# Inverse standard deviations as a power on GpSimd, a second layer's row statistics taken where its input is written, and a minimum in place of an accumulated Relu

## The chip, the cores and the metric

The kernel runs on one core of one Trainium2 chip. The metric is device time in microseconds (us), the median of several executions. Engine names are those of the profile: PE is TensorE (matrix multiply), DVE is VectorE, ACT is ScalarE, POOL is GpSimd, and SP only issues DMAs.

## What is computed

Two graph layers follow each other on `x` of shape (8, 2048, 256) in float32, with one adjacency matrix `adj` (2048, 2048) of integers. Both start from `h = relu(layernorm(x))` and add their result to `x`:

```python
def layer0(x):                      # 4 heads of 64
    h = max(layernorm(x), 0)
    q, k, v = h @ Wq.T + bq, h @ Wk.T + bk, h @ Wv.T + bv
    s = clip(q k^T / 8, -10, 10); s = where(adj == 0, -10, s)
    # softmax over each chunk of 256 keys by itself, chunks added up
    ctx = sum over 8 chunks of softmax(s_chunk) @ v_chunk
    o = ctx @ Wo.T + bo + h
    return x + layernorm(o) * gamma + beta
def layer1(x):                      # 4 heads of 64
    h = max(layernorm(x), 0)
    q = h @ W
    e = leaky_relu(q.a_src + q.a_dst)    # for every pair of rows
    return x + elu(softmax(where(adj > 0, e, -9e15)) @ q)
```

Each layernorm needs, for every row, the mean, the variance and the inverse standard deviation 1/sqrt(variance + 1e-5). There are three of them: of `x` (layer 0's input), of `o` (inside layer 0), and of layer 0's result (layer 1's input). The kernel uses a mask with 0 and 1 in it, and therefore also finds out whether any entry of `adj` is negative; if so, a slower function, `gat_layer`, computes the second layer anew. With the given inputs it doesn't run.

## The kernel before

**Layer 0.** For each of 8 batches `b`, 2048 query rows are cut into four blocks `qb` of 512, and the keys into eight chunks `c` of 256. One (b, qb, c) is a *step*; there are 256. A step multiplies queries with keys on PE (L396, into PSUM buffers `big`, of which there are two), applies clip and mask on DVE (L404, into `E`), takes the exponential on ACT (L410), adds the two key tiles on POOL (L680), sums over keys on PE (L427), weighs the values on PE (L416), and scales the result with the inverse sums on DVE (L452, into `c`, or `acc` in a block's first step). The inverse sums go by way of L434 (copy), a DMA, L441 (reciprocal on DVE), and DMAs through DRAM that spread them over the partitions (`r<-inv`). POOL adds `c` to `acc` (L454).

**Layer 1.** For each batch there are four *passes* (two pairs of heads, two halves of 1024 query rows); a pass has 16 *rounds* `jt` of 128 keys. A round makes two `e` tiles of 128x1024 on DVE (L761), weighs them on PE (L772), scales every other one on ACT (L874), adds the next one to it on POOL (L878), and sums on PE (L784). `e` and `E` share ten buffers. At the end of a pass, `ending` divides and applies elu (L805 to L835).

**Work on the side.** Beside this, generators stand in a list `aside`. Each call of `advance()` lets each generator do a piece; a `yield` without a value ends that call, `yield True` lets the next generator go on. Layer 0 calls `advance` twice a step, layer 1 once a round. So a piece's place in each engine's queue follows from the number of yields before it[...]. If a pass needs what a generator hasn't finished, `drain` runs all that is left of it at once. The generators that matter:
- `make_limit(qb)` makes the mask: `adj` is loaded in eight parts, cast to bf16 on ACT, transposed on PE (L260) and written by DVE (L261).
- `batch(b)` takes row statistics of `x[b]` in `statistics`, then for each block normalizes (L160), transposes (L171), and projects to q, k, v (L297, L191). For batch 0 it does this before the first step, block by block.
- `finish(b, qb, acc)` ends a block of layer 0 during the next block: `o` from `x` (L466, L469), the output projection (L479) added to it (L487), row statistics (`mv2`), normalization (L501), then gamma, beta and `x` on POOL (L512), and a DMA to `x1[b]` in DRAM (L513). `o` has two buffers, which it shares with `for_sums`.
- `preparation(b)` makes what layer 1 needs of batch `b`: statistics, normalized transposed rows, attention terms (L559 to L617, with a trip through DRAM), and eight tiles of `qn` (L191 on PE, L629 on DVE). For batch 0 it runs in the last batch of layer 0; for the others during the passes of the batch before.

**Row statistics** are two DVE instructions a row tile, L47 and L48 in `row_stats`, and give mean and variance in `mv`. Then `roots` and `offsets` make the inverse standard deviation `rstd` and `off = -mean * rstd`: a square root on ACT, a copy with a factor of -1 on ACT, a reciprocal on DVE, a multiplication on POOL (L127, L128, L131, L132). They act on 4 columns (a block) or 16 (a batch). [...]ACT_TABLE_LOAD instructions stand at L127 and at the next exponential.

The functions that the change touches, with the line numbers of the profile:

Of the kernel before, what the change touches and what calls it, by code (L numbers as in the profile page):

```python
# [8 lines left out]
F32 = mybir.dt.float32  # L9
BF16 = mybir.dt.bfloat16  # L10
I32 = mybir.dt.int32
FP8 = mybir.dt.float8e5
AF = mybir.ActivationFunctionType
ALU = mybir.AluOpType
PSUM = bass.MemoryType.PSUM

P = 128
EPS = 1e-5
# [26 lines left out]
def row_stats(nc, small, mv, row):  # L45
    st = small.tile([P, 6], F32, tag="st", name="st")
    nc.vector.bn_stats(st, row)  # L47
    nc.vector.bn_aggr(mv, st)  # L48
# [3 lines left out]
def layers(  # L52
# [18 lines left out]
    nc = tc.nc  # L71
    B, N, F = x.shape
# [4 lines left out]
    NQB = N // QB  # L77
    NKT = N // P
    NCH = N // 256
    NT = QB // P  # L80
    FC = F // P

    const = ctx.enter_context(tc.tile_pool(name="const_l", bufs=1))
    big = ctx.enter_context(tc.tile_pool(name="big", bufs=2))
    small = ctx.enter_context(tc.tile_pool(name="small", bufs=2))
# [27 lines left out]
                coming = load(rows, blk + 1)  # L113
            yield xb

    eps = const.tile([P, 1], F32, tag="eps", name="eps")
    nc.vector.memset(eps, EPS)

    def norms():

        mv = small.tile([P, NKT, 2], F32, tag="mv", name="mv")
        rstd = small.tile([P, NKT], F32, tag="rstd", name="rstd", bufs=3)
        off = small.tile([P, NKT], F32, tag="off", name="off", bufs=3)
        return mv, rstd, off

    def roots(mv, rstd, off, of):
        nc.scalar.activation(rstd[:, of], mv[:, of, 1], AF.Sqrt, bias=eps)  # L127
        nc.scalar.activation(off[:, of], mv[:, of, 0], AF.Copy, scale=-1.0)  # L128

    def offsets(rstd, off, of):  # L130
        nc.vector.reciprocal(rstd[:, of], rstd[:, of])  # L131
        nc.gpsimd.tensor_tensor(off[:, of], off[:, of], rstd[:, of], ALU.mult)  # L132

    def statistics(rows):

        mv, rstd, off = norms()
        for blk, xb in enumerate(ahead(rows)):
            if blk == 0:
                yield True
                yield True  # L140
            for t in range(NT):
                row_stats(nc, small, mv[:, blk * NT + t, :], xb[:, t, :])
                if t % 2:
                    yield True
        of = slice(0, NKT)
        roots(mv, rstd, off, of)
        yield True
        offsets(rstd, off, of)
        yield True
        yield True  # L150
        return rstd, off
# [50 lines left out]
    here = [0]  # L202
# [16 lines left out]


    limit = const.tile([P, NQB, NKT, QB], FP8, tag="limit", name="limit")
    below = const.tile([P, NQB, 2 * NT], F32, tag="below", name="below")
    made = []

    identb = const.tile([P, P], BF16, tag="identb", name="identb")
# [8 lines left out]
    def make_limit(qb):  # L234
        parts = [(t, half) for t in range(NT) for half in range(2)]

        def fetch(k):
            t, half = parts[k]
            q0 = qb * QB + t * P
            raw = adj_in[(qb * len(parts) + k) % 3]  # L240
            nc.sync.dma_start(raw, adj[q0 : q0 + P, half * 1024 : (half + 1) * 1024])
            return raw

        def cast(k):

            m = masks[:, k % 2, :]
            nc.scalar.activation(m, raws[k], AF.Relu, scale=-1.0, accum_out=below[:, qb, k : k + 1])
            nc.scalar.copy(m, raws[k])
            return m

        raws = [fetch(k) for k in range(3)]
        yield True
        m = cast(0)
        yield True
        for k, (t, half) in enumerate(parts):
            if k + 3 < len(parts):
                raws.append(fetch(k + 3))
            ps = aux(BF16).rearrange("p (k q) -> p k q", q=P)
            for j in range(8):
                nc.tensor.transpose(ps[:, j, :], m[:, j * P : (j + 1) * P], identb)  # L260
            nc.vector.tensor_scalar(  # L261
                limit[:, qb, half * 8 : (half + 1) * 8, t * P : (t + 1) * P],
                ps, 0.0, 0.5, ALU.not_equal, ALU.subtract, saturate=False,
            )
            if k + 1 < len(parts):
                m = cast(k + 1)
            else:
                made.append(qb)
            yield
# [49 lines left out]
    def batch(b):  # L319
        qkv[b] = ([], [], [])  # L320
        if b == 0:
            mv, rstd, off = norms()
            norm_of[b] = rstd, off
            for blk, xb in enumerate(ahead(x[b])):
                if blk == 0:
                    yield True
                for t in range(NT):
                    row_stats(nc, small, mv[:, blk * NT + t, :], xb[:, t, :])
                of = slice(blk * NT, (blk + 1) * NT)
                roots(mv, rstd, off, of)  # L330
                offsets(rstd, off, of)
                yield from block(b, blk, xb, *qkv[b])
        else:
            norm_of[b] = yield from statistics(x[b])
            for blk, xb in enumerate(ahead(x[b])):
                yield from block(b, blk, xb, *qkv[b])
# [119 lines left out]
    def finish(b, qb, acc):  # L456
        rstd, off = norm_of[b]
        xb = load(x[b], qb)
        n = here[0]

        while here[0] < n + 1:
            yield False
        o = big.tile([P, NT, F], F32, tag="o", name="o")
        for t in range(NT):
            i = qb * NT + t
            nc.scalar.activation(  # L466
                o[:, t, :], xb[:, t, :], AF.Relu, scale=rstd[:, i : i + 1], bias=off[:, i : i + 1]
            )
        nc.gpsimd.tensor_tensor(o, o, bcast(brow["o"], 1, NT), ALU.add)  # L469
        yield True  # L470
        while here[0] < n + 2:
            yield False
        mv = small.tile([P, NT, 2], F32, tag="mv2", name="mv2")
        for two in range(NT // 2):
            ps = aux().rearrange("p (t f) -> p t f", t=2)
            for u in range(2):
                t = 2 * two + u
                for part in range(2):
                    nc.tensor.matmul(  # L479
                        ps[:, u, :],  # L480
                        acc[:, part, t * P : (t + 1) * P],
                        wT["o"][:, part, :],
                        start=(part == 0),
                        stop=(part == 1),
                    )
            mine = o[:, 2 * two : 2 * two + 2, :]
            nc.vector.tensor_tensor(mine, mine, ps, ALU.add)  # L487
            yield
            for u in range(2):
                t = 2 * two + u  # L490
                row_stats(nc, small, mv[:, t, :], o[:, t, :])
        rstd2 = small.tile([P, NT], F32, tag="rstd2", name="rstd2")
        off2 = small.tile([P, NT], F32, tag="off2", name="off2")
        roots(mv, rstd2, off2, slice(0, NT))
        yield True
        offsets(rstd2, off2, slice(0, NT))
        n = here[0]
        while here[0] < n + 1:
            yield False
        for t in range(NT):  # L500
            nc.scalar.activation(  # L501
                o[:, t, :], o[:, t, :], AF.Identity,
                scale=rstd2[:, t : t + 1], bias=off2[:, t : t + 1],
            )
            if t == 1:
                yield True
        for k, more in enumerate((bcast(brow["gamma"], 1, NT), bcast(brow["beta"], 1, NT), xb)):
            yield True
            n = here[0]
            while here[0] < n + 1:  # L510
                yield False
            nc.gpsimd.tensor_tensor(o, o, more, ALU.add if k else ALU.mult)  # L512
        nc.gpsimd.dma_start(  # L513
            x1[b][qb * QB : (qb + 1) * QB, :].rearrange("(t p) f -> p t f", p=P), o
        )
        yield True


    shared = {}
    least = const.tile([P, B, H], F32, tag="least", name="least")  # L520
    spans = const.tile([P, B, 2 * H], F32, tag="spans", name="spans")

# [21 lines left out]
    def preparation(b):  # L544

        w, wa = shared["w"], shared["wa"]
        norm = yield from statistics(x1[b])

        er = const.tile([P, NQB, P], F32, tag="wv", name="er")
        hTs = []  # L550
# [73 lines left out]
        for blk in range(NQB):  # L624
            q = big.tile([P, NT, F], F32, tag="kv", name="qn", bufs=12)
            for two in range(2):
                ps = sides(w, two, hTs[blk])
                n = blk * NT + 2 * two
# [57 lines left out]
    for n in range(-2, len(steps)):  # L686
# [4 lines left out]
        if n >= 0:  # L691
            b, qb, c = steps[n]
# [160 lines left out]
    for s, (k, jt) in enumerate(rounds):  # L853
        here[0] = len(steps) + s // 4
        b, hp, half = passes[k]
# [46 lines left out]
    nc.vector.tensor_reduce(worst[:, 0:1], spans, mybir.AxisListType.XY, ALU.max)  # L902
    nc.vector.tensor_reduce(worst[:, 1:2], least, mybir.AxisListType.XY, ALU.min)
    nc.vector.tensor_reduce(worst[:, 2:3], inverse_most, mybir.AxisListType.X, ALU.max)
    nc.vector.tensor_reduce(worst[:, 3:4], below, mybir.AxisListType.XY, ALU.max)
    for k, (bound, op) in enumerate(
        ((60.0, ALU.is_gt), (-12.0, ALU.is_lt), (1e26, ALU.is_gt), (0.0, ALU.is_gt))
    ):
        nc.vector.tensor_scalar(bad[:, k : k + 1], worst[:, k : k + 1], bound, None, op)
    ps = aux()  # L910
# [290 lines left out]
```

## Time and profile before

| | |
|---|---|
| median of 3 executions | 4478.36 us (4476.7 to 4484.94) |
| the profiled execution | 4470.84 us, of which the span of instructions 4469.0 us |
| busy share of the span | PE 95%, POOL 73%, DVE 71%, ACT 61% |
| granted PE clock | 0.991 |
| ACT_TABLE_LOAD | 95 of 1283 ns |
| DMA | 262 MB, mean 59 GB/s |
| layer 0, with its start | to about 2903 us |
| layer 1 | from there to 4469 us |

Shares are means over stages with different limits. PE's busy time is modelled, since matmuls are pipelined and their ends are not recorded. The page's groups are written `line engine operation out<-in xcount | busy us, mean ns of one | idle us of the engine just before, and what ended it`.

### The profile page before, as it was taken

To read this page: it belongs to the slowest core of one execution; us is meant where nothing else is said; L and a number is where in the kernel's file an instruction comes from. 1 tells how busy PE (TensorE), PEld (TensorE's weight loads), DVE (VectorE), ACT (ScalarE), POOL (GpSimd) and SP (SyncE) were. 2 spreads that over 40 slices of the span, in tenths; PEclk is the share of its full clock that TensorE was granted. 3 is DMA by queue.
4 is the path that set the end of the run, shared out by engine and by line. 5 is a ranking of instruction groups with operands and counts; after the bars stand their busy time and mean duration, and the time that the engine had idled before them with its cause. 6 is when DMAs were issued, how large, how long until landed. Compare 5 with 4: busy or idle time off the path is not lost. (4 is left out here: it accounts for less than half of the span.)

```text
span 4469.0 us, 73769 instructions
## 1 busy us (share of the span) xinstructions
PE 4235.0 (95%) x28598; PEld 1462.8 (33%) x28598; DVE 3157.1 (71%) x3736; ACT 2712.5 (61%) x3454; POOL 3275.9 (73%) x1558
## 2 busy tenths in 40 slices
PE   6799999999999999999999999989999999999998
PEld 3233333323323333333333333323233332323332
DVE  1775566566565565575565566588989889898987
ACT  4766556656655665665656557565647566565755
POOL 0477787787677777777777777777877777787877
PEclk8999999999999999999999999999999999999999
DMA  2421121111121121121111122121221212122111
GB/s 70 140 62 44 43 66 47 43 56 56 35 64 54 37 66 44 46 64 44 47 55 50 40 64 61 44 100 50 72 63 60 78 57 86 52 74 62 59 55 35
DMA packets 295000, 262.03 MB, mean 59 GB/s; under 512 B 96240, under 2 KB 245488, under 8 KB 294640
## 3 DMA queue, kind: packets, MB, share of 16 engines
q1 hardware_dynamic: 290032, 240.45, 18.8%
q0 software_dynamic: 4608, 16.78, 1.0%
q8 instruction: 226, 3.70, 0.3%
q14 instruction: 134, 1.10, 0.1%
HBM read 218.83 MB, written 36.18 MB: 57 GB/s over the span
## 5 line engine op out<-in xcount | busy, mean ns | idle before, releaser
L680 POOL TENSOR_TENSOR add<-E 128x1024 f32<-128x1024 f32 x512 | 1201.3, 2369 | 721.9 <-PE sums L427 532.1
L410 ACT ACTIVATE E<-E 128x1024 f32<-128x1024 f32 x1024 | 1080.5, 1057 | 827.3 <-DVE E L404 809.6
L404 DVE SCALAR_TENSOR_TENSOR E<-big,limit 128x1024 f32<-128x1024 f32 x1024 | 1203.7, 1217 | 521.6 <-PE big L396 515.5
L761 DVE SCALAR_TENSOR_TENSOR e<-near,far,limit 128x1024 f32<-128x1024 f32 x1024 | 1240.0, 1273 | 23.2 <-ACT near L750 9.8
L878 POOL TENSOR_TENSOR t<-t,e 128x1024 f32<-128x1024 f32 x448 | 1054.4, 2387 | 246.0 <-ACT t L874 210.4
L416 PE MATMUL both<-E,v 128*32 128x512 f32 x8192 | 1037.7, 601 | 59.8 <-DVE c L452 42.3
L772 PE MATMUL acc<-e,qn 128*32 128x512 f32 x8192 | 1060.7, 597 | 24.4 <-DVE e L761 13.5
L396 PE MATMUL big<-qT,kT 64*128 64x512 f32 x4096 | 1032.3, 620 | 11.8 <-DVE E L404 11.8
L874 ACT ACTIVATE t<-e,quot 128x1024 f32<-128x1024 f32 x512 | 561.2, 1142 | 313.5 <-PE den L784 173.0
L396 PEld LDWEIGHTS big<-qT,kT 64*128 64x128 f32 x4096 | 351.6, 187 | 572.0 <-issue 348.8
L454 POOL TENSOR_TENSOR acc<-acc,c 128x1024 f32<-128x1024 f32 x224 | 532.9, 2379 | 3.6 <-DVE c L452 3.6
L452 DVE TENSOR_TENSOR c<-both,r 128x1024 f32<-128x1024 f32 x224 | 274.2, 1224 | 345.9 <-PE both L416 157.1
L416 PEld LDWEIGHTS both<-E,v 128*32 128x32 f32 x8192 | 214.7, 109 | 752.3 <-issue 572.8
L772 PEld LDWEIGHTS acc<-e,qn 128*32 128x32 f32 x8192 | 259.2, 109 | 591.5 <-issue 451.1
L784 PE MATMUL den<-t,for_sums 128*32 128x512 f32 x2048 | 347.6, 595 | 30.6 <-POOL t L878 29.8
L427 PE MATMUL sums<-add,ones 128*32 128x512 f32 x2048 | 269.1, 592 | 0.2 <-POOL add L680 0.2
L434 ACT COPY s<-sums 128x512 f32<-128x512 f32 x256 | 148.4, 580 | 75.5 <-PE sums L427 71.3
L784 PEld LDWEIGHTS den<-t,for_sums 128*32 128x32 f32 x2048 | 79.2, 110 | 223.1 <-issue 113.3
L191 PE MATMUL aux<-w,hT 128*128 128x256 f32 x512 | 127.6, 392 | 22.6 <-DVE qn L629 22.6
L160 ACT ACTIVATE h<-x,off,rstd 128x256 f32<-128x256 f32 x256 | 139.2, 593 | 4.3 <-DMA x<-in_x_dram 2.3
L297 PE MATMUL aux<-hT,wq 128*128 128x512 f32 x256 | 135.7, 658 | 2.7 <-ACT hT L172 2.7
L479 PE MATMUL aux<-wo,acc 128*128 128x256 f32 x512 | 128.2, 393 | 0.0
(117 smaller groups left out, 3033.8 us busy)
## 6 DMA issues: line engine op xcount, KB each, us to landing
r<-inv SPq DMA_DIRECT2D x1024, 64.0 KB
x<-in_x_dram SPq DMA_DIRECT2D x92, 512.0 KB
x<-x SPq DMA_DIRECT2D x64, 512.0 KB
es<-er SPq DMA_DIRECT2D x64, 512.0 KB
adj_in<-in_adj_dram SPq DMA_DIRECT2D x32, 512.0 KB
x<-o POOLq DMA_DIRECT2D x32, 512.0 KB, 3.9
xh<-x SPq DMA_DIRECT2D x64, 256.0 KB
out_dram<-xh SPq DMA_DIRECT2D x64, 256.0 KB
```

What stands on the lines that cost most here:

```text
L396: nc.tensor.matmul(ps[:, hh, :], ks[kt // NT][own, hp, (kt % NT) * P : (kt % NT + 1) * P], qs[qb][own, hp, :], start=True, stop=True,)
L404: nc.vector.scalar_tensor_tensor(e, ps, -0.5, bcast(limit[:, qb, kt, :], 1, 2), ALU.max, ALU.min)
L410: nc.scalar.activation(e, e, AF.Exp, scale=0.25 * EDGE)
L416: nc.tensor.matmul(both[32 * h : 32 * h + 32, part, :], vs[kt // NT][:, kt % NT, mine], es[h // 2][:, h % 2, :], start=first, stop=not first,)
L452: nc.vector.tensor_tensor(to, both, bcast(r, 1, 2), ALU.mult)
L454: nc.gpsimd.tensor_tensor(acc, acc, to, ALU.add)
L680: nc.gpsimd.tensor_tensor(both, first[hp], second[hp], ALU.add)
L761: nc.vector.scalar_tensor_tensor(e, near[hh], far[:, jt, h : h + 1], limit[:, 2 * half : 2 * half + 2, jt, :], ALU.max, ALU.min,)
L772: nc.tensor.matmul(acc[32 * q : 32 * q + 32, blk, :], qn[jt // NT][:, jt % NT, hp * P + 32 * q : hp * P + 32 * q + 32], es[q // 2][:, blk, :],
L784: nc.tensor.matmul(den[32 * q : 32 * q + 32, :], for_sums[:, m, 2 * hp + q // 2, :], ts[q // 2][:, q % 2, :], start=(m == 0 and k == 0), s ...
L874: nc.scalar.activation(t, now[hh], AF.Copy, scale=quot[:, jt // 2, h : h + 1])
L878: nc.gpsimd.tensor_tensor(ts[hh], ts[hh], now[hh], ALU.add)
```

## The change

Three edits. First, `roots` makes `rstd` and `off` on POOL alone: it adds epsilon, raises to the power -0.5 (the exponent is a constant tile of one column, read again for each column), multiplies the mean by -1, and multiplies by `rstd`. `offsets` is gone, and with it one yield in `statistics`. Second, `finish` takes the statistics of layer 0's result from the SBUF tile `o`, one step after the last L512, into a tile `moments` that holds all batches; `preparation` no longer loads `x1[b]` for statistics and begins with `roots`. Third, the cast of `adj` no longer counts negative entries with an accumulating Relu on ACT; DVE takes the minimum of each part, and the end of the kernel compares the smallest with 0.

```diff
-    eps = const.tile([P, 1], F32, tag="eps", name="eps")
-    nc.vector.memset(eps, EPS)
+    power = const.tile([P, 1], F32, tag="power", name="power")
+    nc.vector.memset(power, -0.5)
...
     def roots(mv, rstd, off, of):
-        nc.scalar.activation(rstd[:, of], mv[:, of, 1], AF.Sqrt, bias=eps)
-        nc.scalar.activation(off[:, of], mv[:, of, 0], AF.Copy, scale=-1.0)
-
-    def offsets(rstd, off, of):
-        nc.vector.reciprocal(rstd[:, of], rstd[:, of])
+        nc.gpsimd.tensor_scalar(rstd[:, of], mv[:, of, 1], EPS, None, ALU.add)
+        nc.gpsimd.tensor_tensor(rstd[:, of], rstd[:, of], power.broadcast_to([P, of.stop - of.start]), ALU.pow)
+        nc.gpsimd.tensor_scalar(off[:, of], mv[:, of, 0], -1.0, None, ALU.mult)
         nc.gpsimd.tensor_tensor(off[:, of], off[:, of], rstd[:, of], ALU.mult)
...
@@ statistics
-        of = slice(0, NKT)
-        roots(mv, rstd, off, of)
-        yield True
-        offsets(rstd, off, of)
+        roots(mv, rstd, off, slice(0, NKT))
         yield True
         yield True
...
@@ make_limit, cast
-            nc.scalar.activation(m, raws[k], AF.Relu, scale=-1.0, accum_out=below[:, qb, k : k + 1])
             nc.scalar.copy(m, raws[k])
+            nc.vector.tensor_reduce(
+                below[:, qb, k : k + 1], raws[k], mybir.AxisListType.X, ALU.min
+            )
...
@@ finish, after the DMA to x1
         yield True
+        n = here[0]
+        while here[0] < n + 1:
+            yield False
+        for t in range(NT):
+            row_stats(nc, small, moments[:, b, qb * NT + t, :], o[:, t, :])
+            if t % 2:
+                yield True
...
+    moments = const.tile([P, B, NKT, 2], F32, tag="moments", name="moments")
...
@@ preparation
-        norm = yield from statistics(x1[b])
+        rstd, off = norms()
+        roots(moments[:, b], rstd, off, slice(0, NKT))
+        norm = rstd, off
+        yield True
```

In the first batch and in `finish`, the calls of `offsets` are dropped as well. `mv` is now a tile of its own with one buffer, `below` holds integers, and at the end one more reduction and one copy of a single column bring the smallest entry to the comparison.

More of the change, by code (lines that the diff above doesn't have):

```diff
@@ L114, in ahead @@
             yield xb
-    eps = const.tile([P, 1], F32, tag="eps", name="eps")
-    nc.vector.memset(eps, EPS)
+    power = const.tile([P, 1], F32, tag="power", name="power")
+    nc.vector.memset(power, -0.5)
     def norms():
-        mv = small.tile([P, NKT, 2], F32, tag="mv", name="mv")
         rstd = small.tile([P, NKT], F32, tag="rstd", name="rstd", bufs=3)
         off = small.tile([P, NKT], F32, tag="off", name="off", bufs=3)
-        return mv, rstd, off
+        return rstd, off
     def roots(mv, rstd, off, of):
-        nc.scalar.activation(rstd[:, of], mv[:, of, 1], AF.Sqrt, bias=eps)
-        nc.scalar.activation(off[:, of], mv[:, of, 0], AF.Copy, scale=-1.0)
-    def offsets(rstd, off, of):
-        nc.vector.reciprocal(rstd[:, of], rstd[:, of])
+        nc.gpsimd.tensor_scalar(rstd[:, of], mv[:, of, 1], EPS, None, ALU.add)
+        nc.gpsimd.tensor_tensor(rstd[:, of], rstd[:, of], power.broadcast_to([P, of.stop - of.start]), ALU.pow)
+        nc.gpsimd.tensor_scalar(off[:, of], mv[:, of, 0], -1.0, None, ALU.mult)
         nc.gpsimd.tensor_tensor(off[:, of], off[:, of], rstd[:, of], ALU.mult)
     def statistics(rows):
-        mv, rstd, off = norms()
+        rstd, off = norms()
+        mv = small.tile([P, NKT, 2], F32, tag="mv", name="mv", bufs=1)
         for blk, xb in enumerate(ahead(rows)):
@@ L221, in layers @@
     limit = const.tile([P, NQB, NKT, QB], FP8, tag="limit", name="limit")
-    below = const.tile([P, NQB, 2 * NT], F32, tag="below", name="below")
+    below = const.tile([P, NQB, 2 * NT], I32, tag="below", name="below")
     made = []
@@ L321, in batch @@
         if b == 0:
-            mv, rstd, off = norms()
+            rstd, off = norms()
+            mv = small.tile([P, NKT, 2], F32, tag="mv", name="mv", bufs=1)
             norm_of[b] = rstd, off
@@ L330, in batch @@
                 roots(mv, rstd, off, of)
-                offsets(rstd, off, of)
                 yield from block(b, blk, xb, *qkv[b])
@@ L495, in finish @@
         yield True
-        offsets(rstd2, off2, slice(0, NT))
         n = here[0]
@@ L546, in preparation @@
         w, wa = shared["w"], shared["wa"]
-        norm = yield from statistics(x1[b])
+        rstd, off = norms()
+        roots(moments[:, b], rstd, off, slice(0, NKT))
+        norm = rstd, off
+        yield True
         er = const.tile([P, NQB, P], F32, tag="wv", name="er")
@@ L904, in layers @@
     nc.vector.tensor_reduce(worst[:, 2:3], inverse_most, mybir.AxisListType.X, ALU.max)
-    nc.vector.tensor_reduce(worst[:, 3:4], below, mybir.AxisListType.XY, ALU.max)
+    lowest = small.tile([P, 1], I32, tag="lowest", name="lowest", bufs=1)
+    nc.vector.tensor_reduce(lowest, below, mybir.AxisListType.XY, ALU.min)
+    nc.vector.tensor_copy(worst[:, 3:4], lowest)
     for k, (bound, op) in enumerate(
-        ((60.0, ALU.is_gt), (-12.0, ALU.is_lt), (1e26, ALU.is_gt), (0.0, ALU.is_gt))
+        ((60.0, ALU.is_gt), (-12.0, ALU.is_lt), (1e26, ALU.is_gt), (0.0, ALU.is_lt))
     ):
```

## The prediction

> **What bounds the kernel.** I read the page first, then the windows of whole passes, then the chain of waits inside one pass, then the order of VectorE (DVE). From the page, busy tenths in 40 slices:
>
> ```profile
> PE   6799999999999999999999999989999999999998
> DVE  1775566566565565575565566588989889898987
> POOL 0477787787677777777777777777877777787877
> ```
>
> TensorE (PE) looks full from start to end. DVE changes: 5 to 7 tenths in layer 0 (to about 2903 us), 8 to 9 in layer 1. PE's nines prove little, since its matmul ends are modelled; I therefore look at how time divides where the work is periodic. In layer 1 a batch is four passes of 16 `jt` rounds. Four passes of one batch, then a pass of the last batch, which prepares nothing (columns: stretch, length, busy PE, PEld, DVE, ACT, POOL, clock, DMA share, GB/s):
>
> ```profile
> 3305.80:3355.70 49.90, 46.91 (x368) 12.59 (x363) 47.85 (x69) 25.99 (x30) 40.33 (x20) 1.00 0.28 85
> 3355.70:3397.80 42.10, 40.71 (x364) 13.38 (x368) 39.97 (x37) 34.45 (x48) 34.70 (x18) 1.00 0.31 101
> 3397.80:3442.20 44.40, 43.22 (x404) 13.88 (x400) 41.37 (x40) 32.33 (x45) 37.42 (x21) 1.00 0.20 53
> 3442.20:3499.90 57.70, 54.36 (x408) 23.01 (x404) 45.64 (x46) 26.97 (x34) 39.84 (x20) 1.00 0.13 37
> 4318.10:4360.40 42.30, 40.08 (x340) 11.59 (x332) 39.83 (x37) 25.55 (x30) 37.56 (x18) 1.00 0.18 51
> ```
>
> A bare pass is 42.3 us with DVE at 39.8. The first pass of a batch is 7.6 us longer at about the same number of matmuls (368 against 340), and the fourth 15.4 us longer. Inside the first, the timeline of DVE, and the chain of waits from 3330 to 3350 us:
>
> ```profile
> 3325.55 2.46 DVE L761 SCALAR_TENSOR_TENSOR e<-near,far,limit 128x1024 f32<-128x1024 f32 x2
> 3327.94 0.42 DVE L47 BATCH_NORM_STATS2 st<-x 128x6 f32<-128x256 f32 x1
> ...
> 3329.02 2.44 DVE L761 SCALAR_TENSOR_TENSOR e<-near,far,limit 128x1024 f32<-128x1024 f32 x2
> ...
> 3332.45 2.44 DVE L761 SCALAR_TENSOR_TENSOR e<-near,far,limit 128x1024 f32<-128x1024 f32 x2
> by line: DVE e L761 57.5%; issue 24.1%; DVE st L47 20.1%; DVE mv L48 7.2%
> ```
>
> DVE never idles here: two `e` and two row statistics every 3.43 us, where a round without them takes 2.4. The statistics stand on the path with their full length. So **layer 1 is bound by DVE**. Layer 0 is not: a plain step (start of one L452 to the next) takes 8.4 us with gapless matmuls and DVE at 6, and a step with two more PE units takes 12.24 us whatever DVE and ACT hold.
>
> **What the Trainium skill says.**
> - Perfetto Trace Analysis, Identifying the Most-Contended Engine: matmul busy time is not a good measure, since pipelined matmuls overlap. The trace agrees: PE is 95% busy in a bare pass that DVE paces.
> - ScalarE: Activation LUTs, What ACT_TABLE_LOAD costs: 1283 ns, plus 1380 ns of drain, at each switch of table set. The load agrees (1283 ns below); the drain is not to be seen here, since the instruction before ended at 1213.65 us and the load began at 1213.66.
> - VectorE: DVE Perf Modes, the perf-mode tier table: `tensor_reduce` has a 1x mode only, so 1024 elements are paid one by one.
> - GPSIMD Engine Reference, Elementwise: no price for a power; 2.6 cycles per element of a two-input add (2.37 us for 1024 here) and 12 per element for branching on data.
>
> The rows used:
>
> ```profile
> L127 ACT ACT_TABLE_LOAD x47 | 60.3, 1283 | 0.8
> L410 ACT ACT_TABLE_LOAD x40 | 51.3, 1283 | 0.7
> L132 POOL TENSOR_TENSOR off<-off,rstd 128x4 f32<-128x4 f32 x36 | 7.4, 206 | 85.2 <-DVE rstd L131 85.2
> L132 POOL TENSOR_TENSOR off<-off,rstd 128x16 f32<-128x16 f32 x15 | 3.4, 224 | 58.8 <-PE den L784 51.4 <-DVE rstd L131 7.4
> L571 DVE TENSOR_REDUCE ends<-er 128x1 f32<-128x512 f32 x8 | 5.3, 668 | 0.0
> ```
>
> **Part 1, statistics moved.** The order of the two built programs shows where they go. DVE's count of row statistics is unchanged (384), but 112 of them, those for batches 1 to 7, leave layer 1; 8 (the last two blocks of the last batch) come at its start.
> - *Layer 1, batches 1 to 6.* Gone: 8 rounds x (3.43 - 2.4) = 8.2 us. As the preparation starts about 12 rounds earlier, its eight `qn` steps (L629) stand one to a round in the third pass, where four of them were run in one go by a drain (a round of 11.3 us, 2.2 us a step). The interleaved ones cost 1.3 to 2.2 us, mean 1.8, so 4 x 0.4 = 1.6 us more. Next bound: PE in those rounds, then DVE's 42 us a pass, then POOL's 38. Sum 9.8 x 6 = **-59**.
> - *Batch 0 of layer 1*: -8.2, four late pairs +4.2, drain -1: **-5**.
> - *Last batch of layer 0*: batch 0's 16 rows leave steps that they stretch by about 1.2 us each: **-5**.
> - *DMAs*: 32 of the 64 `x<-x` loads of 512 KB go; the DMA share of the passes is 0.13 to 0.31. The rest of the preparation (four loads, six small DMAs, `roots` on POOL) moves a pass ahead, past the `es`, `xh` and `out` DMAs of other rounds on SP, which now and before wait there for POOL; the place within a pass is much the same. Zero, 2 us a batch if an `x` load is caught behind an `out`.
> - *Layer 0*: two pairs of rows for each of 30 blocks, after the reciprocal (L441) in the block's first step and after the c (L452) that ends it. At 1.08 us a pair this could be 65 us. But in the first slot DVE waits for PE anyway, 0.73 to 3.2 us in every block:
>
> ```profile
> 755.17 0.24 DVE L441 RECIPROCAL sum<-sum 128x16 f32<-128x16 f32 x1
> ...
> 756.14 2.36 DVE L404 SCALAR_TENSOR_TENSOR E<-big,limit 128x1024 f32<-128x1024 f32 x2 [0.73 <-PE big L396]
> ```
>
> and in the second slot PE has the L479 matmuls between. The step at 244.6 us already has such a pair there: it takes 9.83 us, its like without one 9.82. Also new: DVE now waits for POOL's last L512; it ends 3 to 9 us before the slot. I take 0.2 us a block and 1 us in the six blocks where statistics of the next batch sit in the same slot: **+12**; ends 0 and +65.
> - *Buffer*: `o` (two buffers) lives until these statistics. Since `for_sums` takes one earlier than before, the last two blocks' L466 on ACT now wait for DVE, with exponentials queued behind: 3 us each, **+6**; ends 0 and +15.
>
> **Part 2, power on GpSimd.** 94 of 95 table loads go (121 us of ACT), 102 small ACT activations and 51 DVE reciprocals; 153 small POOL instructions come. ACT is 52 to 82% busy in the passes above, and in layer 0 steps with a load are as long as those without (12.24 and 9.82), because PE bounds them; only steps of the six statistics batches show an excess, 0.3 to 1.6 us: **-6**. POOL pays three more instructions of 0.21 us and the power. Of the power no row exists: at least a multiply's 0.21/0.22; with the skill's 12 cycles, 16 x 12 / 1.2 GHz = 0.16 us more, an estimate of 0.4. I take 0.4; an upper end cannot be had from the page. Behind it in POOL's queue stand L680 (layer 0) and L878 (layer 1), on which PE's sums wait. Cover: the step with the four-column power lasts 10.9 to 12.24 us and holds 3 x 2.37 = 7.1 us of POOL work, so 4 us are free; at the start of a batch POOL sits idle for 4.7 to 6.8 us in the timeline (waiting for DVE's L807 or ACT's L874). So zero up to about 4 us for 4 columns and 5 us for 16, in full above that.
>
> **Part 3, minimum.** ACT loses 32 x (1.045 + 0.187) us, DVE gains 32 reductions of 1024: from 0.41 us for 256 and 0.67 for 512, 1.2 us each. Until 116.7 us DVE is busy for 20 us only, and the ACT work stands between `h` and `hT`: 4 blocks x 1.15, plus 3 x 0.85 for the roots that no longer cross four engines, plus 1: **-8**. From 116.7 to 244.6 us, 24 reductions make DVE the bound: 7 steps x 6.1 + 24 x (1.2 + 1.1) = 98 us against 93.4 now: **+7**; ends -5 and +20. The SP queue's mask loads now wait for DVE too, one reduction later.
>
> **Sum.** -59 - 5 - 5 + 12 + 6 - 6 - 8 + 7 = -58 us. The profiled execution took 4470.84 us (span 4469.0); the median shown is 4478.36, 7.5 us above. The change goes onto the median: 4420 us.
>
> **Rivals.**
> - *Layer 1 is PE's after all* (95.5% in every window): the -59 vanishes, about 4480. Against it: `e` rounds follow DVE's own sum. 5%.
> - *The moved pairs cost their full length in layer 0*: +65 for +12, about 4473. Against it: the 9.83 us step. 7%.
> - *The power is slow*, the case on the other side. With p us for 4 columns and 4p for 16, the 15 wide ones exceed their cover by 15 x (4p - 5) and eat the 58 us at p about 2.2; the 36 narrow ones follow from p = 4. At p = 4: 4478 - 58 + 165 = 4585 us, with L680 and L878 late. For it: no row; against it: POOL's other elementwise work runs at a few cycles an element. 10%.
> - *The change doesn't take the table loads away*: excluded, the built program has one.
>
> **Chances.** 0.2% (9 us) is about what a measurement of this kernel can tell from no change. Main case 78%, 4375 to 4460. With the rivals: faster 0.80, same 0.06, slower 0.14. The range reaches to 4490, past the first two rivals; slow powers beyond it are left out.
>
> **What would show it.** Right: first passes at 42 us, none with a round of 11 us, a batch of 184 instead of 194 us; one table load; powers under 1 us; the step after each block's first unchanged at 9.82 or 12.24. Wrong: first passes still at 50 (PE), steps with the new pairs at 11 us, or POOL instructions of several us at the power's line with L680 late behind them.

## The result and the profile after

| | before | after |
|---|---|---|
| median of 6 executions, us | 4478.15 | 4440.09 |
| lowest and highest, us | 4474.9, 4484.94 | 4434.26, 4445.28 |
| profiled execution (span), us | 4470.84 (4469.0) | 4443.6 (4441.7) |
| ACT_TABLE_LOAD | 95 | 1 |
| layer 1 from its first `e`: batch 0, us | 203.2 | 207.4 |
| each of batches 1 to 6, us | 194.1 | 188.6 |
| batch 7 and the end, us | 192.7 | 193.3 |

The change makes the kernel **38 us faster** (ratio 0.9913, 95% interval 0.99 to 0.9926); 58 had been forecast. Line numbers are now those of the changed kernel: `e` is L768, the weighing L779, the scaling on ACT L881, the adds on POOL L885, the sums on PE L791, `roots` L126 to L129, the exponential L407, `o` from `x` L463 and L466. The experiments have line numbers of their own.

The page's busy tenths, against those shown of before: in layer 1 (the last fourteen slices) DVE has two nines instead of five, and POOL eight digits over 7 instead of three.

```profile
PE   6799999999999999999999999989999999999998
DVE  2976666566666675675666566668888898888897
POOL 0477787787777787877777788777888788788797
```

The windows of one batch's four passes and of a bare pass after (columns as before: stretch, length, busy PE, PEld, DVE, ACT, POOL, clock, DMA share, GB/s):

```profile
3494.00:3542.00 48.00, 44.61 (x388) 14.12 (x392) 40.12 (x36) 32.00 (x44) 42.95 (x24) 1.00 0.31 89
3542.00:3586.80 44.80, 43.64 (x408) 13.98 (x400) 41.36 (x40) 32.30 (x45) 37.81 (x21) 1.00 0.19 53
3586.80:3642.40 55.60, 55.60 (x416) 22.88 (x412) 45.63 (x46) 26.96 (x34) 41.90 (x21) 1.00 0.12 39
3642.40:3682.60 40.20, 38.19 (x328) 11.92 (x320) 39.85 (x36) 25.81 (x29) 33.10 (x16) 1.00 0.21 53
4291.10:4333.70 42.60, 40.27 (x340) 11.73 (x340) 39.82 (x36) 25.91 (x30) 37.86 (x19) 1.00 0.16 50
```

DVE's busy time in the first pass fell from 47.85 to 40.12 us, with its statistics gone, but the pass only from 49.9 to 48.0. The engine that is now busiest there after PE is POOL: 42.95 us against 40.33 before. The third and fourth pass together fell from 102.1 to 95.8 us, and the round of 11.3 us is gone; the second, into which the preparation has moved, rose from 42.1 to 44.8 us. So the gain of the moved statistics is there on DVE, and something else holds the first pass up. The groups of POOL and DVE that are new:

```profile
L127 POOL TENSOR_TENSOR rstd<-rstd,power 128x16 f32<-128x16 f32 x15 | 43.9, 2929 | 1.3
L127 POOL TENSOR_TENSOR rstd<-rstd,power 128x4 f32<-128x4 f32 x36 | 37.5, 1041 | 3.0
L243 DVE TENSOR_REDUCE below<-adj_in 128x1 int32<-128x1024 int32 x32 | 38.6, 1206 | 1.9 <-DMA adj_in<-in_adj_dram 1.9
```

The minimum costs the 1.2 us that the prediction took for it. The power costs 1.04 us for 4 columns and 2.93 us for 16, against 0.4. Where the wide one stands is in the timeline of POOL in that first pass (start, duration, and in brackets the idle time before and what ended it):

```profile
3503.40 4.73 POOL L885 TENSOR_TENSOR t<-t,e 128x1024 f32<-128x1024 f32 x2 [4.58 <-ACT t L881]
3508.21 0.26 POOL L126 TENSOR_SCALAR rstd<-moments 128x16 f32<-128x16 f32 x1
3508.56 2.93 POOL L127 TENSOR_TENSOR rstd<-rstd,power 128x16 f32<-128x16 f32 x1
3511.55 0.28 POOL L128 TENSOR_SCALAR off<-moments 128x16 f32<-128x16 f32 x1
3511.91 0.22 POOL L129 TENSOR_TENSOR off<-off,rstd 128x16 f32<-128x16 f32 x1
3512.09 4.70 POOL L885 TENSOR_TENSOR t<-t,e 128x1024 f32<-128x1024 f32 x2
...
3526.61 18.77 POOL L885 TENSOR_TENSOR t<-t,e 128x1024 f32<-128x1024 f32 x8
```

The idle time of 4.58 us comes *ahead* of `roots` in POOL's queue. `roots` needs nothing but `moments`, which layer 0 has written, and still starts only at 3508.21 us, behind the two L885 that had waited: the queue is taken in order. From 3503.40 us to the end of that run at 3545.4 us POOL has no gap of more than 0.1 us. The timeline of DVE in the same pass shows who pays: DVE, which did not idle in the stretch shown of before, waits for POOL to give back `e` buffers.

```profile
3524.09 3.67 DVE L768 SCALAR_TENSOR_TENSOR e<-near,far,limit 128x1024 f32<-128x1024 f32 x3 [0.58 <-POOL t L885]
3529.03 1.28 DVE L768 SCALAR_TENSOR_TENSOR e<-near,far,limit 128x1024 f32<-128x1024 f32 x1 [1.28 <-POOL t L885]
3531.36 8.43 DVE L768 SCALAR_TENSOR_TENSOR e<-near,far,limit 128x1024 f32<-128x1024 f32 x7 [1.04 <-POOL t L885]
```

Adding up POOL in such a pass: 14 adds x 2.36 + 4 endings x 1.28 + 3.9 for `roots` (3508.21 to 3512.09) = 42.1 us, and with the wait of 4.6 us ahead of it 46.7 us, for a pass of 48.0 us. In the chain of waits from 3515 to 3540 us POOL's L885 has 41.4% and PE's L779 21.8%; PE's sums (L791) wait for POOL three times, 0.78 to 1.21 us each, and after 3531.4 us PE has no gap until the pass is over. So POOL seems to set the pace up to there; the experiments try it.

At the start of layer 1 there is a second new wait. The timeline of ACT there:

```profile
2913.15 1.15 ACT L881 ACTIVATE t<-e,quot 128x1024 f32<-128x1024 f32 x1 [0.28 <-DVE e L768]
2922.27 2.08 ACT L463 ACTIVATE o<-x,off,rstd 128x256 f32<-128x256 f32 x4 [7.97 <-DVE st L47]
```

The last block's L463 waits 7.97 us for row statistics (L47) of the block before, with the L881 of the next rounds queued behind it. The first pass of batch 0 ("pass 0" below) lasts 60.0 us; it was 51.4 before.

### The profile page after: what moved, and what is told of

It reads as the page before. It is cut to its first block, busy times and chain, and to the rows that moved or that the text cites. A ratio compares the mean times of both kernels' runs of the same rounds, so it can differ in the third digit from the quotient of the medians.

```text
span 4441.7 us, 73740 instructions
## 1 busy us (share of the span) xinstructions
PE 4216.5 (95%) x28598; PEld 1463.3 (33%) x28598; DVE 3185.7 (72%) x3718; ACT 2543.8 (57%) x3194; POOL 3384.0 (76%) x1711
## 5 line engine op out<-in xcount | busy, mean ns | idle before, releaser
L407 ACT ACTIVATE E<-E 128x1024 f32<-128x1024 f32 x1024 | 1082.8, 1058 | 969.8 <-DVE E L401 949.6
L768 DVE SCALAR_TENSOR_TENSOR e<-near,far,limit 128x1024 f32<-128x1024 f32 x1024 | 1239.9, 1275 | 47.2 <-POOL t L885 26.4
L885 POOL TENSOR_TENSOR t<-t,e 128x1024 f32<-128x1024 f32 x448 | 1054.0, 2386 | 237.2 <-ACT t L881 189.8
L779 PE MATMUL acc<-e,qn 128*32 128x512 f32 x8192 | 1040.4, 596 | 6.1 <-DVE e L768 5.9
L881 ACT ACTIVATE t<-e,quot 128x1024 f32<-128x1024 f32 x512 | 561.9, 1142 | 291.7 <-PE den L791 187.4
L449 DVE TENSOR_TENSOR c<-both,r 128x1024 f32<-128x1024 f32 x224 | 274.2, 1224 | 362.7 <-DMA r<-inv 193.7
L779 PEld LDWEIGHTS acc<-e,qn 128*32 128x32 f32 x8192 | 261.8, 110 | 521.8 <-issue 482.8
L791 PE MATMUL den<-t,for_sums 128*32 128x512 f32 x2048 | 367.2, 599 | 67.3 <-POOL t L885 66.5
L791 PEld LDWEIGHTS den<-t,for_sums 128*32 128x32 f32 x2048 | 78.3, 110 | 284.9 <-POOL t L885 182.3
L155 ACT ACTIVATE h<-x,off,rstd 128x256 f32<-128x256 f32 x256 | 139.2, 593 | 11.3 <-POOL off L129 8.8
```

Source lines behind the costliest of these rows:

```text
L407: nc.scalar.activation(e, e, AF.Exp, scale=0.25 * EDGE)
L449: nc.vector.tensor_tensor(to, both, bcast(r, 1, 2), ALU.mult)
L768: nc.vector.scalar_tensor_tensor(e, near[hh], far[:, jt, h : h + 1], limit[:, 2 * half : 2 * half + 2, jt, :], ALU.max, ALU.min,)
L779: nc.tensor.matmul(acc[32 * q : 32 * q + 32, blk, :], qn[jt // NT][:, jt % NT, hp * P + 32 * q : hp * P + 32 * q + 32], es[q // 2][:, blk, :],
L791: nc.tensor.matmul(den[32 * q : 32 * q + 32, :], for_sums[:, m, 2 * hp + q // 2, :], ts[q // 2][:, q % 2, :], start=(m == 0 and k == 0), s ...
L881: nc.scalar.activation(t, now[hh], AF.Copy, scale=quot[:, jt // 2, h : h + 1])
```

## The experiments

Three theories stood for the first passes: POOL's queue with the wide power in it (1), the preparation's blocks with their loads and transposes (2), PE (3). Each of the eight kernels was timed in turn with the kernel before; ratios are to it. This was done in three sessions, in which the kernel before had medians of 4477.87 us (E1, E2, E3, P1), 4477.24 (E4, P2, P3) and 4474.32 (E5), so medians of different sessions are compared by their ratios. Passes and batches are measured in each kernel's trace from one pass's first `e` to the next; "first pass" is that of batches 1 to 6.

| kernel | median, us | ratio (95%) | pass 0 | first pass | batches 1 to 5 | batch 6 |
|---|---|---|---|---|---|---|
| before | 4478.15 | 1 | 51.4 | 49.9 | 194.1 | 194.1 |
| after | 4440.09 | 0.9913 (0.99 to 0.9926) | 60.0 | 48.0 | 188.6 | 188.6 |
| E1 wide power twice | 4463.48 | 0.9971 (0.9962 to 0.9981) | 63.3 | 51.3 | 192.0 | 192.0 |
| E2 roots in layer 0 | 4411.72 | 0.9842 (0.9828 to 0.9857) | 55.9 | 44.1 | 184.7 | 184.7 |
| E3 = E2, last two blocks late | 4402.79 | 0.9831 (0.9818 to 0.9844) | 46.8 | 44.1 | 184.7 | 190.3 |
| E4 = E3 without the minimum | 4410.0 | 0.9853 (0.9837 to 0.9868) | 46.8 | 44.1 | 184.7 | 190.3 |
| E5 = E2, last block but one late | 4399.46 | 0.9828 (0.9815 to 0.9842) | 46.8 | 44.1 | 184.7 | 189.2 |
| P1 moved statistics alone | 4428.79 | 0.9893 (0.988 to 0.9906) | 57.2 | 45.3 | 184.9 | 184.9 |
| P2 minimum alone | 4475.53 | 0.9997 (0.9989 to 1.0005) | 51.8 | 49.9 | 194.2 | 194.1 |
| P3 power alone | 4464.99 | 0.9973 (0.9961 to 0.9984) | 51.4 | 49.9 | 192.6 | 192.6 |

### E1: the wide power twice

```diff
@@ preparation
         rstd, off = norms()
+        nc.gpsimd.tensor_scalar(rstd, moments[:, b, :, 1], EPS, None, ALU.add)
+        nc.gpsimd.tensor_tensor(off, rstd, power.broadcast_to([P, NKT]), ALU.pow)
         roots(moments[:, b], rstd, off, slice(0, NKT))
```

> The changed kernel, with the 128x16 add and power of each layer 1 preparation issued twice (the first pair writes into off, which is overwritten later; the output is the same). Theory 1: in the first pass of a batch POOL, not DVE, now sets the pace, and what stands in its queue before the t adds is paid. The extra pair is 0.26 + 2.93 us plus gaps, so each of the six preparations in the batches 0 to 5 and the last one (pass 24) adds about 3 us to the first pass of its batch (48.0 to about 51 us): 7 x 3 = +21 us, about 4461 us, with the rounds jt 10 to 15 longer. Theory 2: the first pass is long because of the blocks of the preparation (loads of x behind other transfers, transposes on PE), POOL only follows: the extra pair is covered by the 4.6 us that POOL waits before it, first passes stay at 48.0, about 4440 us. Theory 3: PE bounds these passes: no change either, 4440 us.

Measured: 4463.5 us, 23 us above the changed kernel, and first passes of 51.3 instead of 48.0 us. `roots` with the extra pair holds POOL for 7.2 us instead of 3.9 (timeline of POOL in E1: from 3507.35 to 3514.58 us). The 3.3 us more on POOL come out as 3.3 us more of the pass. That is theory 1; the wait ahead of `roots` covers nothing, against theory 2. One other thing differs, the granted TensorE clock in these passes (the third figure from the end; it is 1.00 in the changed kernel):

```profile
3493.20:3544.40 51.20, 46.64 (x388) 14.34 (x392) 40.35 (x36) 32.22 (x44) 45.97 (x26) 0.93 0.27 83
```

The windows of the six first passes have 0.93 in four and 0.97 in two, and all six take 51.2 or 51.3 us. So the lower clock doesn't set their length.

### E2: no wide power in layer 1

```diff
@@ finish, after the moved row statistics
+        own = moments[:, b]
+        roots(own, own[:, :, 1], own[:, :, 0], slice(qb * NT, (qb + 1) * NT))
...
@@ preparation
-        rstd, off = norms()
-        roots(moments[:, b], rstd, off, slice(0, NKT))
-        norm = rstd, off
+        norm = moments[:, b, :, 1], moments[:, b, :, 0]
```

> The changed kernel, with the roots of layer 1's statistics taken block by block in layer 0, right after the moved row statistics (in place in moments), so that no wide power and none of its three small companions is left at the head of a first pass. 128 more small POOL instructions, 1.7 us a block, in layer 0. Theory 1: the 3.9 us on POOL go from the head of the first pass, which falls from 48.0 to 44 us or somewhat less, a batch from 188.7 to about 184.5 us: 6 to 7 x 4 = -25 us, nothing in layer 0 (the steps have 4 us of free POOL time): about 4415 us. Theory 2 and 3: first passes stay at 48, 4440 us. If the extra narrow powers are not covered in layer 0, its steps after a block's end grow by up to 1.7 us, 30 x 1.7 = +50 us at most.

Measured: 4411.7 us, 28 us below the changed kernel; first passes 44.1 us, 3.9 less, the duration of `roots` again. That is against theories 2 and 3. Batches take 184.7 us, where the prediction had 184. The timeline of POOL in E2 has no `roots` in its place:

```profile
3486.29 9.44 POOL L885 TENSOR_TENSOR t<-t,e 128x1024 f32<-128x1024 f32 x4 [4.58 <-ACT t L881]
3495.68 1.28 POOL L839 TENSOR_TENSOR z<-z 128x512 f32<-128x512 f32 x1
```

The wait of 4.58 us has stayed, so it never belonged to `roots`. Nor is a cost of 32 more narrow powers to be seen in layer 0:

```profile
L127 POOL TENSOR_TENSOR rstd<-rstd,power 128x4 f32<-128x4 f32 x36 | 37.5, 1041 | 3.0
L127 POOL TENSOR_TENSOR moments<-moments,power 128x4 f32<-128x4 f32 x32 | 33.3, 1040 | 2.7
```

From the third block of layer 0 to the end of its last batch but one, a block takes 86.84 us in E2, 86.99 in the changed kernel and 86.66 in E1, whose program is the changed kernel's there. The power is thus not too slow for POOL; it stood where POOL had no time.

### E3 and E5: the wait at the start of layer 1

E3 is E2 with the statistics of blocks 2 and 3 of the last batch back in its preparation; E5 does so for block 2 alone (`==` instead of `>=`).

```diff
@@ finish, before the moved row statistics
+        if b == B - 1 and qb >= NQB - 2:
+            return
...
@@ preparation, for each block blk
+            if b == B - 1 and blk >= NQB - 2:
+                own = moments[:, b]
+                for t in range(NT):
+                    row_stats(nc, small, own[:, blk * NT + t, :], xb[:, t, :])
+                    if t % 2:
+                        yield True
+                roots(own, own[:, :, 1], own[:, :, 0], slice(blk * NT, (blk + 1) * NT))
+                yield True
```

> The kernel e2, with the row statistics of the last two blocks of layer 0's last batch left in the preparation that reads them (pass 24 to 26) instead of in finish: these two o buffers come free at their store, as before the change. Theory on the start of layer 1: the 60.0 us first pass comes from o<-x of the last block, which waits on ACT for the statistics of the block before because for_sums has taken one of the two buffers; without them the first pass falls by 8 to 12 us to about 50 us, against 4 pairs of row statistics more in pass 24 (+4.2 us at DVE's full price). Net -4 to -8 us against e2. Rival: the first pass is long because the last blocks' ending and preparation 1's blocks meet; then it keeps 56 us or more (only the 4.2 us of DVE go) and the total stays within 2 us of e2.

Measured for E3: 4402.8 us, 9 below E2, with intervals of the two ratios that overlap. The traces of layer 1 are clearer: it takes 1506.8 us in E2 and 1499.8 in E3. Pass 0 falls from 55.9 to 46.8 us, where the rival kept 56; batch 6, in which those statistics now stand, grows from 184.7 to 190.3.

> The kernel e3, with only the last block but one of layer 0's last batch left to the preparation that reads it; the statistics of the very last block go back to finish, late in the first pass of layer 1. It parts the two things that e3 took out of that pass together, the wait of o<-x for a buffer and the four pairs of row statistics. Theory (the wait): o<-x of the last block finds a free buffer as in e3, so the pass pays only two late pairs: 46.8 + 2 x 1.1 = 49 us, and the preparation of pass 24 to 26 has two pairs less, -2.2 to -2.8 us: total within 2 us of e3's 4402.8. Rival (the late pairs of the last block hold DVE and through it e, PE and POOL): the pass stays at 53 us or more, about 4406 us or more.

Measured for E5: 4399.5 us, and pass 0 at 46.8 us as in E3, below the 49 expected. I had put the last block's two pairs into pass 0; they come in pass 1 (53.4 us in E5, 52.4 in E3). So of the 9.1 us that pass 0 loses against E2, two pairs of block 2 are 2.1 us (two rounds of 3.5 and 3.4 become 2.4), and the wait is the other 7 us (the sixth and seventh round: 4.4 and 9.7 become 2.4 and 4.6). In E2 the granted clock is 0.76 in these two rounds, in E5 1.00; how much of the 7 us is the wait itself, and how much the lower clock that comes with it, is not parted. The timeline of ACT in E5 shows that `o` of the last block no longer waits:

```profile
2900.79 1.15 ACT L891 ACTIVATE t<-e,quot 128x1024 f32<-128x1024 f32 x1 [0.28 <-DVE e L778]
2901.84 2.06 ACT L463 ACTIVATE o<-x,off,rstd 128x256 f32<-128x256 f32 x4
```

The theory holds against its rival: one block's statistics out of the way, and the wait is gone, while the last block's own stay in `finish`. E3 and E5 cannot be told apart by their times (layer 1 takes 1499.8 and 1500.5 us), and the interval of E2 overlaps both; all three beat the kernel before and the changed kernel. **E5 has the lowest median of the study**, 1.7% below the kernel before.

### P1, P2, P3: each part alone

P1 adds to the kernel before only the second edit (`moments`, with `roots` on ACT and `offsets` on DVE in the preparation), P2 only the third, P3 only the first; the diffs are those of the change.

> The kernel before with the moved row statistics alone: roots stay ACT's square root, DVE's reciprocal and a POOL multiply, negative entries stay with ACT. Theory 1 (wide power on POOL): batches 1 to 6 at 184 to 185 us as the prediction had it, since POOL has only one 0.22 us multiply at the head of the first pass: -57 us there, layer 0 +12 and batch 0 +4, so about 4478 - 41 = 4437 us, no slower than the whole change though two of its parts are missing. Theory 2 and 3: batches stay at 188.7 us as in the whole change, about 4478 - 17 = 4461 us.

> The kernel before with the minimum alone: ACT's 32 Relu sums over the adjacency go, 32 DVE reductions of 1.2 us come. The prediction's terms for it: 4 x 1.15 us off the prologue (the first step of layer 0 starts about 5 us sooner) and +7 us from there to 244.6 us where DVE is the bound: +2 us, about 4480 us. If the whole change's slow start (9.4 us ahead at the first step, 4.1 us at the ninth) comes from the minimum, this kernel loses 5 us between the first step and the ninth; if it comes from the moved statistics, nothing.

> The kernel before with the power alone: statistics of layer 1 stay in layer 1 with their rows loaded again, the 16-column roots are four POOL instructions of 3.9 us together, table loads go. Theory 1: at the head of the preparation's blocks (after the 16 rows, in the second pass of a batch) POOL has slack, since DVE still sets the pace there with its row statistics: layer 1 within 0.5 us a batch of before (194.2 us); layer 0 as the prediction has it, -6 us for table loads and -3 us in the prologue: about 4469 us. If the wide power costs its full 3.9 us in any pass: +27 us more, about 4496 us. If layer 0's 0.8 us narrow power is not covered: 36 x 1.0 = +36 us.

Measured: P1 -49 us, P2 -2 (its interval holds no change), P3 -12. Together that is -63, and the whole change gives -38: **the parts cost each other about 25 us**. E2, which has all three but no wide power in layer 1, gives -66, so nearly all of this is the wide power. P1 came out 8 us better than expected, P2 and P3 some 4 us each.

P1's batches are 184.9 us, so the moved statistics alone bring what was forecast for a batch. P2 starts its first step (a step starts with its L452, L449 in the changed kernel) at 133.5 us instead of 140.7, and its eighth, called the ninth in what was expected, at 231.9 instead of 234.1: it gains 7.2 us in the prologue and gives 5.0 back, so the slow start seems to go with the minimum (the first step differs by 3.9 us between two traces of one program, the changed kernel and E1).

In P3 `roots` stands across the end of a first pass (at 3355.2 us), behind the 16 rows. The timeline of POOL there, with P3's own lines (L871 is the add, L127 to L130 are `roots`):

```profile
3347.18 4.70 POOL L871 TENSOR_TENSOR t<-t,e 128x1024 f32<-128x1024 f32 x2 [0.42 <-DVE e L754]
3352.85 0.26 POOL L127 TENSOR_SCALAR rstd<-mv 128x16 f32<-128x16 f32 x1 [0.96 <-DVE mv L48]
3353.19 2.93 POOL L128 TENSOR_TENSOR rstd<-rstd,power 128x16 f32<-128x16 f32 x1
...
3362.12 4.73 POOL L871 TENSOR_TENSOR t<-t,e 128x1024 f32<-128x1024 f32 x2 [5.35 <-ACT t L867]
```

The same four instructions stand *in front* of an idle gap here: 5.35 us of it are left behind them, and the next add waits for ACT, not for `roots`. The first pass is as long as before (49.9 us) and the second 0.5 us longer (42.7). So `roots` is covered in P3 and paid with 3.9 us in the changed kernel, where it stands behind the gap. Not tried: the whole change with `roots` issued before the adds that end the gap.

### E4: the minimum undone in the better kernel

E4 is E3 without the third edit; `below` and the comparison at the end go back too and are not shown.

```diff
@@ make_limit, cast
+            nc.scalar.activation(m, raws[k], AF.Relu, scale=-1.0, accum_out=below[:, qb, k : k + 1])
             nc.scalar.copy(m, raws[k])
-            nc.vector.tensor_reduce(
-                below[:, qb, k : k + 1], raws[k], mybir.AxisListType.X, ALU.min
-            )
```

> The kernel e3 with negative entries found by ACT's Relu sums again, as before the change (the minimum undone). From the prediction's terms: prologue +5 us, the DVE-bound steps to 244.6 us -7 us: -2 us, within 5 us of e3. It is also the candidate for the fastest kernel, if the minimum costs more than that on DVE.

Measured: 4410.0 us, 7 above E3, where 2 below had been expected; the intervals of the two ratios overlap. In the traces the first step starts at 138.9 us instead of 130.7 and the eighth at 232.7 instead of 229.1, so 3.6 us are seen in their place; the rest is within what layer 0 varies. The minimum does no harm; that it gains is not shown.

## Why the prediction was right, and where it was off

The sum said -58 us and the medians say -38. The direction and the source of the gain were right, the cover of the wide power was wrong, and several smaller sizes were off in both directions. Of the signs named in advance, the one table load and the missing round of 11 us came; first passes of 42 us (48.0), batches of 184 (188.6) and powers under 1 us (1.04 and 2.93) didn't. By its steps:

- **Layer 1 is bound by DVE, and moving the statistics frees it.** Right for the first passes: P1 has 184.9 us a batch against 194.1 before, 6 x 9.2 = -55 us for the -59 of the sum. But two misses cancel in this, which is luck: the first pass gives 4.6 us and not 8.2 (it takes 45.3 us, with 5.0 in its last round, where transposes of the preparation (L171) stand between the weighings on PE), and the other three passes together give 4.6 instead of 1.6.
- **The cover of the wide power.** This is the step that failed: "at the start of a batch POOL sits idle for 4.7 to 6.8 us in the timeline", and so no cost up to 5 us for 16 columns. The idle time is real (4.58 us after), but it stands ahead of `roots` in the queue and cannot be used by it. Behind `roots` POOL has no gap. Where it does have one there, in P3, the cover held. With 2.93 us the power was inside the stated cover and cost its full length all the same, with its three companions 3.9 us in each of seven passes: 7 x 3.9 = 27 us, about what E2 gets back (28 us). "POOL's 38" was named as the third bound, but neither the wait ahead nor the new instructions were added to it; with both it is 46.7 us.
- **The size of the power.** 0.4 us were taken, 1.04 and 2.93 measured. The estimate made from a page of the Trainium skill (GPSIMD Engine Reference, Elementwise: 12 cycles an element for branching on data) gave 0.16 us for 16 columns; the two widths give (2.93 - 1.04) / 12 = 0.157 us for *each* column, so the measurement decides, and that price doesn't carry over to a power. The narrow power at 1.04 us stayed within its cover of 4 us in layer 0, as said: E2 nearly doubles their number at no cost that is seen.
- **The rival on the other side** (a slow power) had the right engine and lines. Its deciding point, p = 2.2 us for four columns, was not reached: p is 1.04, and 16 columns cost 2.8p and not 4p.
- **Batch 0 of layer 1.** -5 was said, and +3 for the one buffer wait that falls there, -2 in sum; +4.2 was measured. The wide power accounts for 4.1 (pass 0 falls from 60.0 to 55.9 us in E2), and the buffer wait for up to 7 us instead of 3 (E5). With these sizes the sum is -5 + 4.1 + 7 = 6.1, and 1.9 us are not explained.
- **Buffer `o`.** Found, but for the wrong number of blocks: the last block waits 7.97 us on ACT, where 3 us each had been put on the last two. The last batch of layer 0, from its first step to the first `e`, takes 324.8 us instead of 323.7, against -5 with some of the +12 and 3 of the +6; a difference of this size can't be read from one profile.
- **The moved pairs in layer 0.** Said: 0.2 us a block. From the third block of layer 0 to the end of its last batch but one, the step in which a block's first late pair stands took 10.66 us before and 10.38 after, the next one 10.71 and 10.87. The shorter one comes from the first edit, since it is 10.41 in P3 and 10.76 in P1; P1, where the pairs move alone, has 10.76 and 10.85, and P2, where they don't, 10.79 and 10.76. So the pairs cost 0.2 us a block at most, and the rival of +65 us is out.
- **Prologue and minimum.** -8 and +7 said. The first step starts 9.4 us sooner, the eighth 4.1 us sooner: -9.4 and +5.3. The working for the second was better than its result: it has 98 us against 93.4, which is +4.6 and not +7 (and makes the sum -60); from the first step to the eighth 98.7 us were measured.
- **Table loads.** -6 in layer 0. P3 gains 12 us, of which layer 1 has 6 x 1.5 = 9; its layer 0 is level in the one profile (2908.1 us against 2908.5). Unexpected is that part of the gain came in layer 1: the fourth pass is 2 us shorter in P3 (55.3 against 57.4).

Two readings of the prediction were off without harm: in the windows that it shows, ACT is busy for 47 to 82% and not 52 to 82 (26.97 of 57.7 us in the fourth pass), and PE for 94 to 97% and not 95.5 in every one.

The spans of the profiled runs differ by 27.3 us, the medians by 38: the profiled run of before lay 7.3 us under its median, that of after 3.5 us above. In these two profiles layer 1 is 28.3 us shorter (1532.3 us against 1560.6), where -61 had been forecast. So about 33 us are missing there, 27 of them by the wide power, and the rest of the 38 would have to come from layer 0, for which the sum has +3. Layer 0 differs from run to run by that much: the changed kernel and E1 are the same up to its last batch, which begins at 2584.6 us in one trace and at 2573.6 in the other. Layer 1 begins at 2897.0 to 2909.4 us in the five traces with all three edits (changed kernel, E1, E2, E3, E5), at the latest in the changed kernel's, and at 2908.5 before. Differences of layer 0 under some 10 us can't be read from one profile; the batches 1 to 5 of layer 1 agree to 0.1 us within a trace.

What stays open: whether the minimum gains at all (2 us alone and 7 us in E4's comparison, neither clear of noise), what layer 0 gains by the change, and which of P3's removed instructions shorten its fourth passes. None was tried further; a third buffer for `o` was not tried either.

## What to carry to other kernels

When work is taken from the engine that sets the pace, add up the next engine's whole queue for that stretch, with what the same change puts on it and with the waits that it can't use; two edits that are each good can take back a good part of each other's gain (25 us of 63 here). Idle time is cover only if the new instruction stands in front of it in its engine's queue, so ask on which side of the gap the instruction stands, and not only how long the gap is: here the same `roots` was free in front of a gap (P3) and paid in full behind one. And a small operation on a hidden engine is best placed in the stage that has slack for it, as the powers in layer 0 show.

## What the runs showed of the hardware

A power on GpSimd took 1.04 us for 128x4 and 2.93 us for 128x16 float32; if it grows evenly, an estimate from these two widths, that is some 0.41 us and 0.157 us a column. The narrow one took the same on every other element (1.040 us in E2's `moments`) as on whole tiles (1.041 us). A multiplication of the same shapes took 0.20 and 0.22 us. A minimum over 1024 int32 on VectorE took 1.21 us. The granted TensorE clock was 0.93 or 0.97 in the first passes of E1, in which PE waits longer for POOL (2.88 us at 3517.0 us, against 0.78 to 1.21), and 1.00 in that of the changed kernel.
